# An output projection as two Strassen chunks in the feed-forward's order, its sums from DRAM

## The chip, the cores and the metric

The kernel runs on one NeuronCore of one Trainium2 chip. A NeuronCore has five engines that run side by side, each with its own queue of instructions in order: TensorE (PE, matrix products into PSUM; its weight loads are shown apart as PEld), VectorE (DVE), ScalarE (ACT), GpSimd (POOL) and SyncE (SP), which here only issues DMAs. They wait for each other by semaphores. The metric is the device time of one execution in microseconds (us), as a median of several runs.

## What is computed

A block of a recurrent network on x of 8 batches x 1024 tokens x 512 features, all in fp32:

```python
xn = _layernorm(x, axis=-1)
# attention part, for each batch, scale = 128 ** -0.5
local_out  = softmax(q k^T * scale) v                 # full attention, 128 features
sparse_out = the same, with only the 102 largest scores of a row kept
x_proj     = xn @ memory_proj_w
mem_out    = concat(x_proj, softmax(x_proj bank^T) bank) @ mem_out_w + mem_out_b
pred_out   = gelu((xn @ pred_in_w + pred_in_b) @ pred1_w + pred1_b) @ pred2_w + pred2_b
combined   = concat([local_out, sparse_out, mem_out, pred_out])   # 512 features
s = combined @ warboss_w + warboss_b                  # the output projection
# feed-forward part
g = silu(relu(xn @ w1 + b1) @ w2 + b2)                # 512 -> 2048 -> 512
out = x + s * g
```

The output projection is a product of (tokens x 512) with a weight of 512 x 512.

## The kernel before

**Units of work.** A tile i is 128 tokens, a pair p two tiles (256 tokens, `T`), a group g two pairs. There are 64 tiles, 32 pairs and 16 groups. Attention goes by tiles and pairs, the feed-forward by groups (w1) and pairs (w2).

**Strassen products.** The feed-forward's two products, the q and k projections and the projection `m` (the inputs of memory and prediction heads) are already computed by a Strassen scheme of the Winograd form: both operands are cut into 2 x 2 blocks, 4 sums of blocks are made on each side, 7 products of blocks take the place of 8, and additions put the results together. The sums of the weights are made once by `form_chunk` (L483), written to DRAM, and then read by `load_chunk` (L460) as a chunk of 7 blocks of 128 x 256 numbers (896 KB) into a ring `w` of four buffers. While the weights are raw, the fourth raw block lies in a separate tile, `raw_blocks` (L457). An "up" chunk (w1) is 14 matmuls of 256 columns, a "down" chunk (w2) 7. The left sums of the hidden values are made on POOL by `hidden_sums` (L597, tile hs), at most three chunks ahead; the additions after the products are `add_products` (L508): two of 128x512 and three of 128x256 elements. `use_units` (L548) calls it for the units (up, q, k, m) on POOL and then passes the result on through ACT. At most two units are open (tile u has two buffers). `make_gate` (L618) does it for a pair's w2 product (tile m), adds b2 and applies SiLU.

**The planner.** Which instruction comes when on each engine is laid down when the program is built. `run` (L132) keeps a clock for each engine in columns of TensorE. Attention and all follow-up work are generators ("chains") that yield the clock or the condition at which they go on. Where no chain is due, the next piece of the filler is issued: `feed_forward` (L634) goes through the chunks in the fixed order of `plan` (L400). A chunk that isn't ready holds the whole filler. Chains are sorted by rank: hidden sums -1, units 0, attention 1, the gate and the end of a pair 2. Chains for the n-th tile start at `begin + n * STEP` (L1024, L1034). The order is fixed on each engine, so on the chip an instruction can wait for one before it on its own engine.

**The order of a group.** For g: up g,0 to up g,7; among the first four the second half of the previous odd pair (down 2g-1,4 to 7), among the last four down 2g,0 to 3, and m after up g,2. Then down 2g,4 to 7 and down 2g+1,0 to 3, with the q (and k) chunk of the next group among them. The chunk `down n,7` waits until pair n-1 is "gated".

**The output projection before.** `finish_pair` (L923) takes a pair whose heads are done: LOCAL and SPARSE attention (`attend`, L753) and the memory and prediction heads (2 and 3, started by `two_heads`, L1047). It borrows two tiles of the pool `ws` (`borrow`, L207, 512 KB each), loads warboss_w into them and x into xr on SP's queue, waits for the last head, and runs for each of two token tiles four matmuls of 512 columns into po. ACT copies po to o, POOL adds the bias wb; later, when the gate is there, POOL multiplies, adds x and stores. `joined` is set after the products; the next pair's attention and small heads wait for it (`before_pair`, L766), because each head has one buffer. wk and wq of the start, and each batch's wv, are borrowed from `ws` as well.

Nearly all instructions are issued through one helper (L85), so the profile's rows are told apart by their tiles: f is the w2 product in PSUM, ph_up the w1 product, po the output projection, pa an attention's product with v, sc its scores, pp the prediction head, ptx and ptp transposes.

Of the kernel before, what the change touches and what calls it, by code (L numbers as in the profile page):

```python
# [20 lines left out]
def kernel(  # L21
# [182 lines left out]
    def can_borrow(n):  # L204
        return lambda: lent[0] + n <= 2

    def borrow(name, *parts):  # L207
        lent[0] += 1
        t = sb.tile([P, ND, 2 * HD], F32, tag="ws", name=name, bufs=2)
        at = 0  # L210
        for w in parts:
            v = w.rearrange("(c p) n -> p c n", p=P)
            if v.shape[1] == ND:
                sp.dma_start(out=t[:, :, at : at + v.shape[2]], in_=v)
                at += v.shape[2]
            else:
                t = t.rearrange("p c n -> p (c n)").rearrange("p (c n) -> p c n", n=v.shape[2])
                sp.dma_start(out=t, in_=v)
        return t

    def give_back(n=1):
        lent[0] -= n
# [4 lines left out]
    def borrow_qkv(name, which):  # L227
        return borrow(name, *[w[:, which * HD : (which + 1) * HD] for w in qkv])
# [3 lines left out]
    first_k = borrow_qkv("wk_0", 1)  # L232
# [91 lines left out]
    def ln_apply(b, j, t):  # L324

        mv, rs = stats[b]
        dve.tensor_scalar(t, t, mv[:, j, 0:1], rs[:, j : j + 1], ALU.subtract, ALU.mult)
        on("dve", 330)
        return after("dve")
# [70 lines left out]
    def plan():  # L400

        half = NWC // 2
        for g in range(GROUPS + 1):
            for k in range(NWC):
                if g < GROUPS:
                    yield "up", g, k
                if k >= half and g < GROUPS:  # L410
                    yield "down", 2 * g, k - half
                if k < half and g:
                    yield "down", 2 * g - 1, k + half
                if k == 2 and g < GROUPS:
                    yield "m", g, 0
                if g == 0 and k in (3, 5):
                    yield "form", "qk"[k // 4], 0
            if g < GROUPS:
                for n in range(2):
                    for k in range(half):  # L420
                        yield "down", 2 * g + n, k + half * (1 - n)
                        if g + 1 < GROUPS:
                            at = n * half + k
                            if (g + 1) % NG == 0:
                                if at == 2:
                                    yield "k", g + 2, 0
# [9 lines left out]
        for kind in ("up", "down", "q", "k", "m")  # L436
        for k in range(NWC if kind in ("up", "down") else 1)
# [3 lines left out]
    w2v = ffn_w2.rearrange("(h k p) n -> p h k n", h=2, p=P)  # L441

# [14 lines left out]
    raw_blocks = sb.tile([P, 7, H], F32, tag="m", name="raw_blocks")  # L457
    formed = set()

    def load_chunk(at):  # L460
        if at >= len(order_of_chunks):
            return
        kind, n, k = order_of_chunks[at]
        w = sb.tile([P, 7, H], F32, tag="w", name=f"w_{kind}_{n}_{k}", bufs=4)
        w_tiles[kind, n, k] = w
        what = n if kind == "form" else kind
        if (what, k) in formed:
            sp.dma_start(out=w, in_=w_dram[what, k])
            return
        formed.add((what, k))  # L470
        extra = raw_blocks[:, at % 7]
        raw[at] = what, extra
        if what == "down":
            for slot, h, d in ((0, 0, 0), (1, 1, 0), (6, 1, 1)):
                sp.dma_start(out=w[:, slot], in_=w2v[:, h, k, ts(d, H)])
            sp.dma_start(out=extra, in_=w2v[:, 0, k, H:])
        else:
            u1, u2 = blocks(what, k)
            for slot, v in ((0, u1[:, 0]), (1, u1[:, 1]), (4, u2[:, 1])):
                sp.dma_start(out=halves(w[:, slot]), in_=v)  # L480
            sp.dma_start(out=halves(extra), in_=u2[:, 0])

    def form_chunk(at):  # L483

        if at not in raw:
            return
        kind, n, k = order_of_chunks[at]
        what, extra = raw.pop(at)
        w = w_tiles[kind, n, k]
        if what == "down":  # L490
            on_pool("tensor_sub", w[:, 5], extra, w[:, 0])
            on_pool("tensor_sub", w[:, 2], w[:, 6], w[:, 5])
            on_pool("tensor_sub", w[:, 3], w[:, 6], extra)
            on_pool("tensor_sub", w[:, 4], w[:, 1], w[:, 2])
        else:
            on_dve("tensor_add", w[:, 5], extra, w[:, 4])
            on_dve("tensor_sub", w[:, 2], w[:, 5], w[:, 0])
            on_dve("tensor_sub", w[:, 3], w[:, 0], extra)
            on_dve("tensor_sub", w[:, 6], w[:, 1], w[:, 2])
        sp.dma_start(out=w_dram[what, k], in_=w)  # L500
# [91 lines left out]
    starts = {}  # L592
    units_begun = [0]
    sums_made = [0]
    downs_made = [0]

    def hidden_sums():  # L597

        for _, n, k in [c for c in order_of_chunks if c[0] == "down"]:
            yield lambda: (n, k) in hidden and sums_made[0] < downs_made[0] + 3  # L600
            yield after("act", 0)
            h = hidden.pop((n, k))
            a11, a21, a12, a22 = (h[:, u, ts(j, P)] for u in range(2) for j in range(2))
            s = sb.tile([P, 4, P], F32, tag="hs", name=f"hs_{n}_{k}", bufs=3)
            on_pool("tensor_add", s[:, 0], a21, a22)
            on_pool("tensor_sub", s[:, 1], s[:, 0], a11)
            on_pool("tensor_sub", s[:, 2], a11, a21)
            on_pool("tensor_sub", s[:, 3], a12, s[:, 1])
            operands[n, k] = (a11, a12, s[:, 1], s[:, 2], a22, s[:, 0], s[:, 3])
            sums_made[0] += 1  # L610
            due = after("pool")
            wanted_at[n, k] = due
# [4 lines left out]

    def make_gate(n, m):  # L618
        add, free = (on_dve, lambda: True) if n == LAST else (on_pool, pool_is_free)
# [14 lines left out]
    def feed_forward():  # L634

        sums = []
        for at, (kind, n, k) in enumerate(order_of_chunks):
            if kind == "form":
# [5 lines left out]
                continue  # L644
            if kind != "down":
# [4 lines left out]
                    and n in tokens  # L650
# [16 lines left out]
            for i in range(7):  # L667
                if kind != "down":
                    if i % 2 == 0:
                        ps = ring(f"ph_{kind}_{n}_{k}_{i}", (P, 2, T))  # L670
                    for c in range(2):
                        pe.matmul(
                            ps[:, i % 2], halves(w[:, i])[:, c], tokens[n][i][:, c],
                            start=c == 0, stop=c == 1,
                        )
# [247 lines left out]
    def finish_pair(b, p):  # L923
        yield needs(*[("head", b, p, h) for h in (LOCAL, 2, 3)])
        if (b, p) != (0, 0):
            yield needs(("out", *divmod(b * NP + p - 1, NP)))
        yield can_borrow(2)
        both = [borrow(f"wb_{b}_{p}_{k}", warboss_w[ts(k, T), :]) for k in range(2)]
        xs = [load_x("xr", b, 2 * p + j, "xr") for j in range(2)]
        yield clock["pe"] + AHEAD  # L930
        yield needs(("head", b, p, SPARSE))
        yield after("act")
        order = (LOCAL, 2, 3, SPARSE)
        os = []
        for j in range(2):
            ps = ring(f"po_{b}_{p}_{j}", (P, D))
            accumulate(
                ps,
                [heads[b, p, h][:, ts(j, P)] for h in order],
                [both[h // 2][:, h % 2, :] for h in order],  # L940
                D,
            )
# [7 lines left out]
        yield needs(("gate", b, p))  # L950
        yield after("act")
        late = b * NP + p == LAST
        op, free = (on_dve, lambda: True) if late else (on_pool, pool_is_free)
# [70 lines left out]
    STEP = int(0.995 * (12031 + NWC * (2 * 7 * T + 2 * 7 * H) // 4))  # L1024
# [5 lines left out]
    give_back()  # L1030
# [3 lines left out]
    for n in range(B * NT):  # L1034
# [57 lines left out]
```

## Time and profile before

| | |
|---|---|
| median of 3 runs | 2952.89 us (2951.46 to 2952.97) |
| the profiled execution | 2952.86 us, its span 2951.1 us |
| granted TensorE clock | 0.998 of full speed |
| VectorE: MAX8 and MATCH_REPLACE8 (sparse selection) | 943.1 + 850.5 us in the two largest rows |
| POOL: additions on u_up | 330.3 us (x256 of 128x512, 1290 ns) + 292.9 us (x384 of 128x256, 763 ns) |
| POOL: hs<-h of 128x128 | 245.2 us (x512, 479 ns) |
| TensorE: po<-wb,head of 128x512 | x512, 593 ns each by the page, 230.1 us busy |
| ACT: o<-po of 128x512 | x64, 585 ns |
| DMA | 512.60 MB, mean 174 GB/s; SP's queue 48.0% of the 16 engines |
| DMA wb (warboss_w) | x64, 512 KB, 6.4 us from issue to landing |
| DMA w_down | x248, 896 KB, 4.6 us from issue to landing |

How to read it: a row of the profile names an engine, an operation, output and input tiles, shapes, the number of instructions, busy time and the mean of one. Ends of matmuls are modelled and overlap the next one's start, so the mean duration (593 ns) isn't the spacing. A row of waits reads "engine tile <- the one that released it: total us, times, longest us". The page's slices cut the span into 40 equal parts and give the busy share of each in tenths.

### The profile page before, as it was taken

The page shows a single profiled execution, that of the slowest core. Times are in us where ns is not written, and L with a number is a line of the kernel's source. Part 1 is how long each engine was busy: PE and PEld are TensorE (multiplying, and loading weights), DVE is VectorE, ACT ScalarE, POOL GpSimd, SP SyncE. Part 2 cuts the span into 40 slices and gives each one's busy share as a digit, 9 for nine tenths or more (in the row PEclk, how much of TensorE's full clock was granted, in tenths as well). Part 3 has the DMA queues.
Part 4 walks back from the last instruction along what each step waited for, and adds up shares of the span by engine and source line. Part 5 has one row for each costly group of instructions (what it writes and reads, how often), then busy time and mean ns, then how long its engine had stood idle before and what let it go on. Part 6 is the DMA issues. An engine that isn't in the chain of part 4 may idle for free.

```text
span 2951.1 us, 37099 instructions
## 1 busy us (share of the span) xinstructions
PE 2881.2 (98%) x12912; PEld 2322.4 (79%) x12912; DVE 2369.6 (80%) x3181; ACT 1641.4 (56%) x3106; POOL 1937.4 (66%) x2499
## 2 busy tenths in 40 slices
PE   8999999999999999999999999999999999999998
PEld 5867878777887788778788778787888778777786
DVE  6999878887778787879869787788958979589595
ACT  3556555555565654556546565465654656446463
POOL 3775765767657676566857658576685766847665
PEclk9999999999999999999999999999999999999999
DMA  5764543645436455453554545455444554444544
GB/s 163 252 224 154 185 178 120 219 152 189 174 122 227 142 191 184 146 193 139 191 175 168 190 141 180 175 179 185 154 173 163 195 185 149 175 147 169 179 175 148
DMA packets 139035, 512.60 MB, mean 174 GB/s; under 512 B 13662, under 2 KB 39280, under 8 KB 138848
## 3 DMA queue, kind: packets, MB, share of 16 engines
q1 hardware_dynamic: 133392, 493.01, 48.0%
q0 software_dynamic: 5456, 17.22, 1.6%
q8 instruction: 102, 1.67, 0.2%
q14 instruction: 85, 0.70, 0.1%
HBM read 475.97 MB, written 34.21 MB: 173 GB/s over the span
## 4 chain that ended last, share of the span: by engine, by line
PE 81%; DVE 8%; ACT 5%; POOL 2%; DMA 1%; issue 1%; SPq 0%; POOLq 0%; DVEq 0%; ACTq 0%
PE ph_up L85 22%; PE f L85 21%; PE pa L85 7%; PE po L85 7%; PE sc L85 6%; PE pv L85 4%; PE ptp L85 3%; DVE top L85 3%; DVE left L85 3%; PE ph_m L85 3%; PE ph_k L85 2%; PE ph_q L85 2%; PE pp L85 1%; ACT L85 1%; ACT h L85 1%
## 5 line engine op out<-in xcount | busy, mean ns | idle before, releaser
L85 DVE MAX8 top<-left 128x8 f32<-128x1024 f32 x768 | 943.1, 1228 | 26.7
L85 DVE MATCH_REPLACE8 left<-top,left 128x1024 f32<-128x1024 f32 x704 | 850.5, 1208 | 0.0
L85 POOL TENSOR_TENSOR u_up<-u_up 128x256 f32<-128x256 f32 (+1 forms) x640 | 619.9, 974 | 329.9 <-ACT u_up L85 304.5
L85 PE MATMUL f<-w_down,hs 128*128 128x256 f32 x2048 | 540.8, 381 | 3.8 <-POOL w_down L85 3.1
L85 PE MATMUL ph_up<-t,w_up 128*128 128x256 f32 x2048 | 483.2, 380 | 0.0
L85 PEld LDWEIGHTS f<-w_down,hs 128*128 128x128 f32 x2048 | 383.9, 191 | 71.0 <-issue 18.8
L85 PEld LDWEIGHTS ph_up<-t,w_up 128*128 128x128 f32 x2048 | 385.1, 191 | 65.2 <-issue 17.9
L85 PE MATMUL f<-w_down,h 128*128 128x256 f32 x1536 | 423.9, 381 | 4.8 <-DMA w_down<-w_down_dram 2.3
L85 ACT COPY u_up<-ph_up 128x512 f32<-128x512 f32 (+1 forms) x512 | 264.1, 530 | 238.3 <-PE ph_up L85 237.4
L85 PE MATMUL ph_up<-xnT,w_up 128*128 128x256 f32 x1536 | 383.3, 380 | 1.1 <-ACT el L85 0.9
L85 POOL TENSOR_TENSOR hs<-h 128x128 f32<-128x128 f32 x512 | 245.2, 479 | 164.7 <-PE f L85 144.4
L85 PEld LDWEIGHTS f<-w_down,h 128*128 128x128 f32 x1536 | 287.6, 191 | 57.3 <-issue 15.7
L85 PEld LDWEIGHTS ph_up<-xnT,w_up 128*128 128x128 f32 x1536 | 288.3, 191 | 45.2 <-issue 8.1
L85 DVE MAX8 top<-s 128x8 f32<-128x1024 f32 x64 | 78.3, 1224 | 268.6 <-ACT s L85 268.6
L85 PE MATMUL sc<-kT,qT 128*128 128x512 f32 x512 | 241.6, 595 | 4.1 <-ACT u_up L85 1.9
L85 PE MATMUL pa<-pT,v 128*128 128x256 f32 x1024 | 231.9, 380 | 0.6 <-ACT pT L85 0.6
L85 PE MATMUL po<-wb,head 128*128 128x512 f32 x512 | 230.1, 593 | 0.0
L85 ACT ACTIVATE h<-u_up,biasT 128x256 f32<-128x256 f32 x512 | 219.7, 501 | 8.4 <-POOL u_up L85 8.4
L85 POOL TENSOR_TENSOR o<-o,wb 128x512 f32<-128x512 f32 x64 | 81.5, 1273 | 217.4 <-ACT o L85 217.1
L85 PEld LDWEIGHTS pa<-pT,v 128*128 128x128 f32 x1024 | 194.8, 190 | 27.1 <-ACT pT L85 1.2
L85 ACT COPY pT<-ptp 128x512 f32<-128x512 f32 x256 | 148.5, 586 | 116.1 <-PE ptp L85 115.3
L85 POOL TENSOR_TENSOR m<-m 128x256 f32<-128x256 f32 (+1 forms) x155 | 152.1, 989 | 64.0 <-ACT m L85 59.6
(151 smaller groups left out, 4150.3 us busy)
## 6 DMA issues: line engine op xcount, KB each, us to landing
w_down<-w_down_dram SPq DMA_DIRECT2D x248, 896.0 KB, 4.6
w_up<-w_up_dram SPq DMA_DIRECT2D x120, 896.0 KB, 4.6
wb<-in_L_attn_warboss_w_dram SPq DMA_DIRECT2D x64, 512.0 KB, 6.4
xl<-in_L_attn_x_dram SPq DMA_DIRECT2D x64, 256.0 KB, 4.6
xr<-in_L_attn_x_dram SPq DMA_DIRECT2D x64, 256.0 KB, 2.9
out_dram<-xr POOLq DMA_DIRECT2D x62, 256.0 KB, 2.8
xs<-in_L_attn_x_dram SPq DMA_DIRECT2D x56, 256.0 KB, 4.8
w_q<-w_q_dram SPq DMA_DIRECT2D x15, 896.0 KB, 4.6
```

The lines of the kernel that those rows point to most:

```text
L85: r = made(*args, **kwargs)
```

## The change

The output projection becomes two chunks of kind "po" in the filler's order, each 7 products of 128x128 by 128x256 numbers (e = 0 for the heads 0 and 2, e = 1 for the heads 1 and 3), both summed in PSUM. A pair's po stands after `down n,5` for an even pair (after `down 1,1` for the first) and after `down n,7` for an odd one. The weight's sums come from DRAM like those of the other weights; they are made once, on DVE. `finish_pair` makes the left sums of the heads on POOL and waits for the results; `use_units` does the additions and adds the bias, on POOL, for the last pair on DVE.

Besides: the raw blocks of all weights are loaded into their own chunk and one is overwritten in place (`raw_blocks` is gone); `ws` has one buffer, and wk of the start lies in the memory of el; the q and k weights' sums are formed at other places; `two_heads` waits for ACT before its first matmul; the statistics of the second batch start a step later; the planner allows 500 columns where it allowed 330 for the normalization of a tile; STEP is shorter by 0.995 x 256 columns.

```diff
     def can_borrow(n):
-        return lambda: lent[0] + n <= 2
+        return lambda: lent[0] + n <= 1
...
-        t = sb.tile([P, ND, 2 * HD], F32, tag="ws", name=name, bufs=2)
+        t = sb.tile([P, ND, 2 * HD], F32, tag=tag, name=name)
...
-    first_k = borrow_qkv("wk_0", 1)
+    first_k = borrow_qkv("wk_0", 1, "el")
...
         dve.tensor_scalar(t, t, mv[:, j, 0:1], rs[:, j : j + 1], ALU.subtract, ALU.mult)
-        on("dve", 330)
+        on("dve", 500)
...
-                if g == 0 and k in (3, 5):
-                    yield "form", "qk"[k // 4], 0
+                if k == half - 1 and g:
+                    for e in range(2):
+                        yield "po", 2 * g - 1, e
+                if (g, k) in ((0, 5), (1, 4)):
+                    yield "form", "qk"[g], 0
             if g < GROUPS:
                 for n in range(2):
                     for k in range(half):
                         yield "down", 2 * g + n, k + half * (1 - n)
+                        if (n, k) == (int(g == 0), 1):
+                            for e in range(2):
+                                yield "po", 2 * g, e
...
+    wbv = warboss_w.rearrange("(h k p) n -> p h k n", h=2, p=P)
...
-    raw_blocks = sb.tile([P, 7, H], F32, tag="m", name="raw_blocks")
...
-        if what == "down":
-            for slot, h, d in ((0, 0, 0), (1, 1, 0), (6, 1, 1)):
-                sp.dma_start(out=w[:, slot], in_=w2v[:, h, k, ts(d, H)])
-            sp.dma_start(out=extra, in_=w2v[:, 0, k, H:])
+        if what in ("down", "po"):
+            v = w2v if what == "down" else wbv
+            for slot, h, d in ((0, 0, 0), (1, 1, 0), (3, 0, 1), (6, 1, 1)):
+                sp.dma_start(out=w[:, slot], in_=v[:, h, k, ts(d, H)])
...
+        if what in ("down", "po"):
+            on = on_pool if what == "down" else on_dve
+            on("tensor_sub", w[:, 5], w[:, 3], w[:, 0])
+            on("tensor_sub", w[:, 2], w[:, 6], w[:, 5])
+            on("tensor_sub", w[:, 3], w[:, 6], w[:, 3])
+            on("tensor_sub", w[:, 4], w[:, 1], w[:, 2])
...
     def use_units(kind, g, k, m, nth):
-        for _ in add_products(m, on_pool):
-            yield pool_is_free
+        add, free = engine_for(g if kind == "po" else 0)
+        for _ in add_products(m, add):
+            yield free
+        if kind == "po":
+            n = g
+            if n:
+                yield needs(("out", *divmod(n - 1, NP)))
+            os = outs[n] = []
+            for j, blocks in enumerate((m[:, 1:7:5], m[:, 4:6])):
+                o = sb.tile([P, D], F32, tag="o", name=f"o_{n}_{j}", bufs=2)
+                add("tensor_add", halves(o), blocks, halves(wb))
+                os.append(o)
+                yield free
+            done.add(("units", nth))
+            return
...
+    def left_sums(h1, h2, s):
+
+
+        a11, a21, a12, a22 = (h[:, ts(j, P)] for h in (h1, h2) for j in range(2))
+        on_pool("tensor_add", s[:, 0], a21, a22)
+        on_pool("tensor_sub", s[:, 1], s[:, 0], a11)
+        on_pool("tensor_sub", s[:, 2], a11, a21)
+        on_pool("tensor_sub", s[:, 3], a12, s[:, 1])
+        return (a11, a12, s[:, 1], s[:, 2], a22, s[:, 0], s[:, 3])
...
+    def engine_for(n):
+        return (on_dve, lambda: True) if n == LAST else (on_pool, pool_is_free)
...
+            if kind == "po" and k == 0:
+                wants[0] = lambda: True
+                yield 0
+                load_chunk(at + 3)
+                form_chunk(at + 1)
+                continue
...
                     "constants" in done
-                    and n in tokens
+                    and (
+                        ("po", n) in operands and wanted_at["po", n] <= clock["pe"]
+                        if kind == "po"
+                        else n in tokens
+                    )
                     and (nth < 2 or ("units", nth - 2) in done)
...
-            load_chunk(at + 3)
+            if kind != "po":
+                load_chunk(at + 3)
             form_chunk(at + 1)
             w = w_tiles.pop((kind, n, k))
+            if kind == "po":
+                both = [(w_tiles.pop((kind, n, 0)), w)]
+                both = [(x[:, i], y[:, i]) for x, y in both for i in range(7)]
...
+                        if kind == "po":
+                            lhsT, rhs = operands[kind, n][c][i], both[i][c]
+                        else:
+                            lhsT, rhs = halves(w[:, i])[:, c], tokens[n][i][:, c]
+                        pe.matmul(ps[:, i % 2], lhsT, rhs, start=c == 0, stop=c == 1)
                         yield T
...
                 start(use_units(kind, n, k, m, nth), rank=0)
+                if kind == "po":
+                    load_chunk(at + 3)
+                    operands.pop((kind, n))
+                    done.add(("joined", *divmod(n, NP)))
...
     def finish_pair(b, p):
-        yield needs(*[("head", b, p, h) for h in (LOCAL, 2, 3)])
-        if (b, p) != (0, 0):
-            yield needs(("out", *divmod(b * NP + p - 1, NP)))
-        yield can_borrow(2)
-        both = [borrow(f"wb_{b}_{p}_{k}", warboss_w[ts(k, T), :]) for k in range(2)]
+        n = b * NP + p
+        yield needs(*[("head", b, p, h) for h in range(4)], *before_pair(b, p))
+        yield after("act", 0)
+        sums = sb.tile([P, 2, 4, P], F32, tag="ho", name=f"ho_{n}")
+        operands["po", n] = []
+        for e in range(2):
+            operands["po", n].append(
+                left_sums(heads.pop((b, p, e)), heads.pop((b, p, e + 2)), sums[:, e])
+            )
+            wanted_at["po", n] = after("pool", 100000 * (1 - e))
+            yield after("pool", 0)
+        wanted_at["po", n] = after("pool")
+        if n:
+            yield needs(("out", *divmod(n - 1, NP)))
         xs = [load_x("xr", b, 2 * p + j, "xr") for j in range(2)]
-        yield clock["pe"] + AHEAD
-        yield needs(("head", b, p, SPARSE))
+        yield lambda: ("gate", b, p) in done and len(outs.get(n, ())) == 2
         yield after("act")
-        order = (LOCAL, 2, 3, SPARSE)
-        os = []
-        for j in range(2):
-            ps = ring(f"po_{b}_{p}_{j}", (P, D))
-            accumulate(
-                ps,
-                [heads[b, p, h][:, ts(j, P)] for h in order],
-                [both[h // 2][:, h % 2, :] for h in order],
-                D,
-            )
-            o = sb.tile([P, D], F32, tag="o", name=f"o_{b}_{p}_{j}", bufs=2)
-            copy(o, ps, 360)
-            on_pool("tensor_add", o, o, wb)
-            os.append(o)
-            yield pool_is_free
-        give_back(2)
-        done.add(("joined", b, p))
...
-    STEP = int(0.995 * (12031 + NWC * (2 * 7 * T + 2 * 7 * H) // 4))
+    STEP = int(0.995 * (11775 + NWC * (2 * 7 * T + 2 * 7 * H) // 4))
...
-                start(prepare_stats(b + 1), now + 2000)
+                start(prepare_stats(b + 1), now + (2000 if b else STEP))
...
                 yield needs(("m", b, p), *before_pair(b, p))
+                yield after("act")
```

More of the change, by code (lines that the diff above doesn't have):

```diff
@@ L204, in can_borrow, with borrow @@
     def can_borrow(n):
-        return lambda: lent[0] + n <= 2
-    def borrow(name, *parts):
-        lent[0] += 1
-        t = sb.tile([P, ND, 2 * HD], F32, tag="ws", name=name, bufs=2)
+        return lambda: lent[0] + n <= 1
+    def borrow(name, *parts, tag="ws"):
+        lent[0] += tag == "ws"
+        t = sb.tile([P, ND, 2 * HD], F32, tag=tag, name=name)
         at = 0
@@ L212, in borrow, with give_back, borrow_qkv @@
             v = w.rearrange("(c p) n -> p c n", p=P)
[L213 to L218, printed above, removed]
-        return t
-    def give_back(n=1):
-        lent[0] -= n
+            sp.dma_start(out=t[:, :, at : at + v.shape[2]], in_=v)
+            at += v.shape[2]
+        return t
+    def give_back():
+        lent[0] -= 1
     qkv = (local_qkv_w, sparse_qkv_w)
     AHEAD = 8000
-    def borrow_qkv(name, which):
-        return borrow(name, *[w[:, which * HD : (which + 1) * HD] for w in qkv])
+    def borrow_qkv(name, which, tag="ws"):
+        return borrow(name, *[w[:, which * HD : (which + 1) * HD] for w in qkv], tag=tag)
     first_x = [load_x("xl", 0, j, ("o", "xr")[j // 2]) for j in range(4)]
-    first_k = borrow_qkv("wk_0", 1)
+    first_k = borrow_qkv("wk_0", 1, "el")
     for h in range(2):
@@ L435 @@
         (kind, k): dram.tile([P, 7, H], F32, tag=f"{kind}_{k}", name=f"w_{kind}_{k}_dram")
-        for kind in ("up", "down", "q", "k", "m")
-        for k in range(NWC if kind in ("up", "down") else 1)
+        for kind, ks in (("up", NWC), ("down", NWC), ("po", 2), ("q", 1), ("k", 1), ("m", 1))
+        for k in range(ks)
     }
@@ L470, in load_chunk @@
         formed.add((what, k))
-        extra = raw_blocks[:, at % 7]
-        raw[at] = what, extra
-        if what == "down":
-            for slot, h, d in ((0, 0, 0), (1, 1, 0), (6, 1, 1)):
-                sp.dma_start(out=w[:, slot], in_=w2v[:, h, k, ts(d, H)])
-            sp.dma_start(out=extra, in_=w2v[:, 0, k, H:])
+        raw[at] = what
+        if what in ("down", "po"):
+            v = w2v if what == "down" else wbv
+            for slot, h, d in ((0, 0, 0), (1, 1, 0), (3, 0, 1), (6, 1, 1)):
+                sp.dma_start(out=w[:, slot], in_=v[:, h, k, ts(d, H)])
         else:
             u1, u2 = blocks(what, k)
-            for slot, v in ((0, u1[:, 0]), (1, u1[:, 1]), (4, u2[:, 1])):
+            for slot, v in ((0, u1[:, 0]), (1, u1[:, 1]), (3, u2[:, 0]), (4, u2[:, 1])):
                 sp.dma_start(out=halves(w[:, slot]), in_=v)
-            sp.dma_start(out=halves(extra), in_=u2[:, 0])
     def form_chunk(at):
@@ L487, in form_chunk @@
         kind, n, k = order_of_chunks[at]
-        what, extra = raw.pop(at)
+        what = raw.pop(at)
         w = w_tiles[kind, n, k]
[L490 to L494, printed above, removed]
+        if what in ("down", "po"):
[4 more added lines that the diff above has]
+            on("tensor_sub", w[:, 4], w[:, 1], w[:, 2])
         else:
-            on_dve("tensor_add", w[:, 5], extra, w[:, 4])
+            on_dve("tensor_add", w[:, 5], w[:, 3], w[:, 4])
             on_dve("tensor_sub", w[:, 2], w[:, 5], w[:, 0])
-            on_dve("tensor_sub", w[:, 3], w[:, 0], extra)
+            on_dve("tensor_sub", w[:, 3], w[:, 0], w[:, 3])
             on_dve("tensor_sub", w[:, 6], w[:, 1], w[:, 2])
@@ L592 @@
     starts = {}
+    outs = {}
     units_begun = [0]
@@ L602, in hidden_sums @@
             h = hidden.pop((n, k))
-            a11, a21, a12, a22 = (h[:, u, ts(j, P)] for u in range(2) for j in range(2))
             s = sb.tile([P, 4, P], F32, tag="hs", name=f"hs_{n}_{k}", bufs=3)
[L605 to L609, printed above, removed]
+            operands[n, k] = left_sums(h[:, 0], h[:, 1], s)
             sums_made[0] += 1
@@ L616 @@
     LAST = B * NP - 1
+    def engine_for(n):
+        return (on_dve, lambda: True) if n == LAST else (on_pool, pool_is_free)
     def make_gate(n, m):
-        add, free = (on_dve, lambda: True) if n == LAST else (on_pool, pool_is_free)
+        add, free = engine_for(n)
         for _ in add_products(m, add):
@@ L671, in feed_forward @@
                     for c in range(2):
-                        pe.matmul(
-                            ps[:, i % 2], halves(w[:, i])[:, c], tokens[n][i][:, c],
-                            start=c == 0, stop=c == 1,
-                        )
+                        if kind == "po":
[3 more added lines that the diff above has]
+                        pe.matmul(ps[:, i % 2], lhsT, rhs, start=c == 0, stop=c == 1)
                         yield T
@@ L923, in finish_pair @@
     def finish_pair(b, p):
-        yield needs(*[("head", b, p, h) for h in (LOCAL, 2, 3)])
-        if (b, p) != (0, 0):
-            yield needs(("out", *divmod(b * NP + p - 1, NP)))
-        yield can_borrow(2)
-        both = [borrow(f"wb_{b}_{p}_{k}", warboss_w[ts(k, T), :]) for k in range(2)]
+        n = b * NP + p
[12 more added lines that the diff above has]
+            yield needs(("out", *divmod(n - 1, NP)))
         xs = [load_x("xr", b, 2 * p + j, "xr") for j in range(2)]
-        yield clock["pe"] + AHEAD
-        yield needs(("head", b, p, SPARSE))
+        yield lambda: ("gate", b, p) in done and len(outs.get(n, ())) == 2
         yield after("act")
-        order = (LOCAL, 2, 3, SPARSE)
-        os = []
-        for j in range(2):
-            ps = ring(f"po_{b}_{p}_{j}", (P, D))
-            accumulate(
-                ps,
-                [heads[b, p, h][:, ts(j, P)] for h in order],
-                [both[h // 2][:, h % 2, :] for h in order],
-                D,
-            )
-            o = sb.tile([P, D], F32, tag="o", name=f"o_{b}_{p}_{j}", bufs=2)
-            copy(o, ps, 360)
-            on_pool("tensor_add", o, o, wb)
-            os.append(o)
-            yield pool_is_free
-        give_back(2)
-        done.add(("joined", b, p))
[L950 to L953, printed above, removed]
+        late = n == LAST
+        op, free = engine_for(n)
+        os = outs.pop(n)
         for j, o in enumerate(os):
@@ L1029 @@
         project_k(0, g, LOCAL, first_k)
-    give_back()
     begin = clock["pe"] + 2000
```

## Prediction

> **What bounds the kernel now.** I read the page's busy shares first, then the row of slices, the chain that ended last, and the timeline of TensorE. The busy shares and the slices:
>
> ```profile
> PE 2881.2 (98%) x12912; PEld 2322.4 (79%) x12912; DVE 2369.6 (80%) x3181; ACT 1641.4 (56%) x3106; POOL 1937.4 (66%) x2499
> ...
> PE   8999999999999999999999999999999999999998
> ...
> PE 81%; DVE 8%; ACT 5%; POOL 2%; DMA 1%; issue 1%; SPq 0%; POOLq 0%; DVEq 0%; ACTq 0%
> ```
>
> TensorE is busy in every slice and carries 81% of the chain (third line). The Trainium skill warns against taking that at its word: "Perfetto Trace Analysis", section "Identifying the Most-Contended Engine", calls matmul busy time a bad measure and would judge by weight loads. Those are 79%, beside VectorE's 80% (first line). By that rule TensorE has a fifth in hand and fewer columns might buy nothing. So I look at starts instead of ends, in the timeline of TensorE (start, duration, instruction, count):
>
> ```profile
> 164.58 3.60 PE L85 MATMUL po<-wb,head 128*128 128x512 f32 x8
> ...
> 168.01 0.59 PE L85 MATMUL f<-w_down,hs 128*128 128x256 f32 x2
> ...
> 1469.93 3.62 PE L85 MATMUL pa<-pT,v 128*128 128x256 f32 x16
> 1473.38 2.75 PE L85 MATMUL ph_k<-t,w_k 128*128 128x256 f32 x12
> ```
>
> From the first po to the next f, 3.43 us for 8 instructions: 0.429 us per 512 columns. From pa to ph_k, 3.45 us for 16: 0.216 us per 256 columns. An fp32 matmul is two such instructions (po has 512 = 32 pairs x 8 matmuls x 2). Taking 0.429, 0.216, 0.109 and 0.06 us for the instructions of 512, 256, 128 and 64 columns, the trace's TensorE work sums to 2848 us; the starts exceed it by 83 us in all; 9.7 us lie before the first and 9.6 after the last. **The columns bound it**: the trace decides against the rule. A column removed is worth 0.84 ns per instruction as long as the rest keeps pace.
>
> **The output projection on TensorE.** Removed per pair: 2 x 4 matmuls of 512 columns, 16 instructions x 0.429 = 6.87 us. Added: 7 products x 2 chunks of 256 columns, 28 x 0.216 = 6.05 us. Saved 0.82 us a pair, **26.3 us** over 32. Weight loads rise from 16 to 28 a pair; one lasts 191 ns (the po and pa rows), so it fits under 216 ns, with 25 ns to spare where it had 238. The pa and f rows already run at that spacing, so I charge nothing. If that cover were gone, 12 loads x 0.19 us would be 2.3 us a pair and the gain would turn.
>
> **The same product on the other engines.** Per pair POOL gains 8 left sums of 128x128 (479 ns in the hs row: 3.83 us), 2 adds of 128x512 (1.29 us) and 3 of 128x256 (0.76 us): 4.87 us. The two bias adds (1.27 us) stay. 8.7 us x 32 = 278 us, so POOL goes from 1937 to some 2215 us, 66% to 76%. ACT copies four products' tiles (3 x 0.58 + 0.38) where it copied two (2 x 0.585): +0.95 us a pair, 56% to 58%. Here a rule speaks against the change: "GPSIMD Engine Reference", section "Engine selection", puts elementwise work on VectorE, GpSimd being about 2x slower with two inputs. The trace agrees: 128x512 m<-m takes 1278 ns on POOL and 691 on DVE. By the rule the additions belong on VectorE, where 8.7 us would be about 4.6; but VectorE would then stand at 80% + 5%, in front of the selection rounds, and the price on POOL counts only where TensorE waits for POOL. TensorE's waits show how little that is now:
>
> ```profile
> PE ptx L85 <- DVE xl L85: 19.0, 14, 9.7
> PE pp L85 <- ACT xh L85: 11.1, 12, 1.4
> ...
> PE f L85 <- POOL w_down L85: 3.1, 1, 3.1
> ...
> PE f L85 <- DMA w_down<-w_down_dram: 2.3, 1, 2.3
> ...
> PE f L85 <- POOL hs L85: 0.8, 1, 0.8
> ```
>
> (Columns: total us, times, longest.) POOL's own order also loses a blockage, since the bias add no longer stands at its head waiting for a product just issued:
>
> ```profile
> POOL u_up L85 <- ACT u_up L85: 304.5, 101, 30.6
> ...
> POOL o L85 <- ACT o L85: 217.1, 53, 12.8
> ```
>
> Where can POOL be late? Counting 28 instructions to an up chunk and 14 to a down chunk, I find each chunk's start. Hidden sums end some 10 to 60 us before their chunk, but twice in a group only 1 to 6 us. A chunk's additions and ReLUs end 10 to 16 us after its matmuls, and in the second half of the up loop only 2 to 5 us before the unit after next, because at most two unit tiles are open. po is one more unit, with 7.5 us on POOL against an up chunk's 4.9 us. So the late stretch is after an odd pair's po: up 4 and up 5 have one down chunk less (3.0 us) ahead of them. The nearest row is the memory chunk m, which stands between up chunks in just this way: ph_up's starts exceed their spacing by only 2.7 us in the whole run. Bounds: below, minus 2 us (the blockage gone reaches a few chunks); above, 7.5 - 4.9 = 2.6 us a pair, 84 us. I take the value near the row, 0.25 us a pair: **+8 us**.
>
> **Order and waits.** po stands at a fixed place of the filler. I compared that place with the copies of both attention heads (head<-pa): the chunk before it ends 30 to 98 us after the second head, except for the last pair (6 us). The left sums (3.8 us) fit, so po does not stall the filler. po now comes 12 to 64 us later than before, and `joined` with it. Behind `joined` wait the next pair's two small heads and its attentions. For even pairs these slip 10 to 20 us (pair 16's small heads began at 1563.0, its predecessor's po would end near 1583), yet their own po is 30 us or more off, and the filler runs meanwhile: nothing lost. On ACT the head copies move with them. The gate's wait (`gated` before the next down 7) had some 40 us in hand; about 10 of them go.
>
> The small heads also wait for ACT now, and for `joined`, which for even pairs comes after their input. The wait of pp for xh (11.1 us above) was paid once a group, on the spot; I expect it gone, **-11 us** (ends 0 and -15.8, all excess before pp). What is late next there is the Gelu, 0.5 us in all. The longer allowance for a normalized tile moves a transpose 170 columns (0.28 us) later; 13 of its 14 waits (9.3 us; the one of 9.7 lies at the start) shrink by at most 3.7: **-3 us**.
>
> **DMA and SP.** wb's 64 loads of 512 KB become 64 of 896 KB: +25 MB on 513, 48% to about 50% of the queues' time. SP's issues keep their number. But po takes two ring tiles, and the load three chunks on is issued only when its matmuls end, so two chunks lie ready instead of three. After an even pair's po these are two downs, 6.05 us of TensorE; w_down lands in 4.6 us. It fits unless SP stands at an xr load: SP waited 246.4 us in 54 times for out_dram, 4.6 us each. Ends: 0, and (4.6 + 4.6 - 6.05) x 16 = 50 us; I take 0, as xr's loads come after `out`, tens of us off, and charge it to a rival.
>
> **One answer together.** Weights' sums in place, k and q formed at other places, wk in el's memory, one ws buffer, statistics a step later: once each, on engines that wait anyway; between -3 us (the 3.1 us wait for w_down near 150 us) and +3 us (8 sums for po on DVE, 0.8 us each, in a queue of 2.4 us rounds). I take 0. STEP shrinks by 255 columns, which follows the work and isn't a second gain. The tail: from the last head (2929.0 us) it was 6 us of f, 6.9 of po, then copy, bias, product, sum and the store. After: sums under the same f, 6.05 of po, a copy of 256 columns and DVE adds of 0.4 to 0.7 us. Equal within 1 us.
>
> **The sum.** -26.3 - 11 - 3 + 8 = -32.3. The profiled execution took 2952.86 us (span 2951.1 and 1.8 around it), like the median, 2952.89. So **2921 us**; with the ends of the unknowns near their rows, 2906 to 2934.
>
> **Rivals.**
> - Only the columns count (chance 0.18): the slipped attentions bunch, and new waits eat what pp and ptx give. For it: `joined` falls up to 24 us after the time at which the LOCAL attention now runs (pair 24). Against it: the filler covers. 2952.9 - 26.3 + 8 = 2935; up to 2946 with another 11.
> - POOL becomes late (0.05), after each po. For it: 20 us windows of POOL in the trace reach 98%. Against: its average stays near 76%, and m's row. 2921 - 8 + 84 = 2997. It ends on the other side from 1.3 us lost a pair (40/32).
> - The ring runs dry after even pairs' po (0.04): 2921 + 50 = 2971, from 2.0 us a time.
> - The change removes no time because weight loads set the pace at 256 columns (0.03): against it stand the pa and f rows. About 2950.
>
> My own case has 0.70. Below 0.2% (5.9 us) a measurement of this kernel can't be told from no change. Faster (under 2947): 0.86, my case and 0.16 of the first rival; within: 0.05, its rest and the last; slower: 0.09, the two between. The range goes from 2904 (all of pp's 15.8 us, no new wait) to 2945.
>
> **What would show it.** po as 896 products' instructions at 0.216 us and 6.05 us a pair; pp's wait for xh gone from TensorE's list; POOL near 2215 us and still few waits of PE for POOL hs; `POOL o <- ACT o` gone; f's waits for w_down's DMA still a few us. I am wrong if f or ph_up wait tens of us for POOL or DMA, if weight loads exceed 191 ns, or if TensorE's excess of starts grows past 83 us.

## The result, and the profile after

The changed kernel takes 2927.41 us (median of 4 runs, 2925.8 to 2928.97) beside 2952.93 us of the kernel before (4 runs): a ratio of 0.9915, 95% interval 0.9897 to 0.9932, or 25.5 us less. Forecast were 32 us less, with a range of 2904 to 2945 us. The profiled execution took 2925.8 us, its span 2923.7.

From the page of the changed kernel: the busy shares, a group of POOL's additions, and the row of the w_po loads (number of loads, KB each, median us from issue to landing):

```profile
PE 2856.1 (98%) x13296; PEld 2395.7 (82%) x13296; DVE 2379.2 (81%) x3196; ACT 1668.8 (57%) x3169; POOL 2184.0 (75%) x2908
...
L85 POOL TENSOR_TENSOR u_po<-u_po 128x256 f32<-128x256 f32 (+1 forms) x155 | 148.2, 963 | 18.5 <-ACT u_po L85 12.1
...
w_po<-w_po_dram SPq DMA_DIRECT2D x62, 896.0 KB, 4.7
```

POOL grew by 247 us, weight loads to 82%, and TensorE is as full as it was. What it waits for has changed. Its waits in the changed kernel, first five and the row of pp (total us, times, longest us):

```profile
PE ph_po L85 <- DMA w_po<-w_po_dram: 15.0, 11, 2.1
PE ptx L85 <- DVE xl L85: 11.9, 4, 10.0
PE ptp L85 <- ACT es L85: 7.3, 3, 5.3
PE f L85 <- ACT h L85: 5.8, 2, 4.7
PE pa L85 <- ACT pT L85: 4.4, 4, 1.3
...
PE pp L85 <- ACT pT L85: 0.8, 1, 0.8
```

The wait of pp for xh (11.1 us before) is gone, and ptx waits 4 times instead of 14. At the head stands a new one: the output projection waits for its own weights.

A second view adds up. I take each TensorE instruction's distance to the next one's start, subtract the spacing of its shape (0.429, 0.216, 0.108, 0.06 us for 512, 256, 128, 64 columns) and sum what exceeds it by more than 40 ns, by the instruction that came late:

| us | before | changed kernel |
|---|---|---|
| columns at their spacing | 2847.8 | 2821.9 |
| excess, all | 82.7 | 82.0 |
| of it ahead of pp | 15.8 | 1.1 |
| ahead of ptx | 13.9 | 5.8 |
| ahead of ph_po (po before) | 0.1 | 22.7 |

The time went down by about the columns (25.5 us by the medians, 25.9 us of columns). The two small gains came, 22.9 us together, and the new excess at ph_po took 22.7 us. So the changed kernel gained what the columns alone give, as in the first rival ("only the columns count"), but for another cause and without that rival's 8 us for POOL: it had 2935 us.

**Where ph_po waits.** Counting 28 instructions to a pair, all of the excess lies at even pairs, and but for 0.1 us in 7 of the 16 (4, 8, 10, 12, 16, 22, 26). 16.8 us of it stand ahead of the first matmul of each of the two chunks. One of the seven, pair 8, in the timelines of SP's queue and of TensorE, and in SP's waits between 868 and 895 us:

```profile
877.52 4.15 SPq L85 DMA_DIRECT2D xr<-in_L_attn_x_dram  x2
881.76 0.38 SPq L85 DMA_DIRECT2D xs<-in_L_attn_x_dram  x1
882.24 0.86 SPq L85 DMA_DIRECT2D w_po<-w_po_dram  x2
```

```profile
885.51 1.03 PE L85 MATMUL f<-w_down,hs 128*128 128x256 f32 x4
888.61 0.67 PE L85 MATMUL ph_po<-w_po,head 128*128 128x256 f32 x2 [2.07 <-DMA w_po<-w_po_dram]
890.69 2.93 PE L85 MATMUL ph_po<-w_po,head 128*128 128x256 f32 x6 [1.42 <-DMA w_po<-w_po_dram]
```

```profile
SPq L85 <- DMA out_dram<-xr: 10.8, 2, 7.4
```

SP stands at the two xr loads, whose buffers the stores of the pair before still read: 7.4 us ahead of the first, which leaves at 877.52, and 3.4 ahead of the second, 10.8 us in all. (The 4.15 us of the row run from the first one's start to the second one's end.) Behind them both w_po loads are ready to go and leave one right after the other, at 882.24 and 882.72. One matmul (two instructions) after the first chunk, the second is needed as well. Six of the seven cases show the same rows, SP at xr and then both w_po loads at once; SP's stand at a pair's xr loads was 8.9 to 13.0 us in the seven. In pair 10 two w_down loads leave at once behind xr, and w_po after them.

**A part of it is the clock.** Two stretches of pair 8 (start and end, length, busy us of PE, PEld, DVE, ACT and POOL with their instructions, then granted TensorE clock, DMA share, GB/s):

```profile
877.00:894.00 17.00, 13.52 (x54) 10.84 (x53) 10.36 (x15) 2.81 (x6) 12.75 (x15) 0.90 0.80 291
892.00:894.00 2.00, 2.00 (x6) 1.55 (x6) 0.00 (x0) 0.29 (x1) 0.00 (x0) 0.50 0.93 370
```

Behind the wait the granted clock was 0.50 for 3.4 us, and the matmuls started every 0.427 us instead of 0.216. The same happened in pairs 12 and 22, and in none of the other four. These three pairs had waited longest, 2.8 to 3.8 us within one po, the others up to 2.3 us. The slow matmuls are some 5 of ph_po's 22.7 us.

### The profile page after: what moved, and what is told of

It reads as the page before. It is cut to its first block, busy times and chain, and to the rows that moved or that the text cites. A ratio compares the mean times of both kernels' runs of the same rounds, so it can differ in the third digit from the quotient of the medians.

```text
span 2923.7 us, 38478 instructions
## 1 busy us (share of the span) xinstructions
PE 2856.1 (98%) x13296; PEld 2395.7 (82%) x13296; DVE 2379.2 (81%) x3196; ACT 1668.8 (57%) x3169; POOL 2184.0 (75%) x2908
## 5 line engine op out<-in xcount | busy, mean ns | idle before, releaser
L85 POOL TENSOR_TENSOR u_up<-u_up 128x256 f32<-128x256 f32 (+1 forms) x640 | 618.1, 972 | 247.8 <-ACT u_up L85 223.1
L85 DVE TENSOR_REDUCE nml<-el 128x1 f32<-128x1024 f32 x64 | 77.4, 1209 | 231.3 <-ACT el L85 231.0
L85 ACT ACTIVATE h<-u_up,biasT 128x256 f32<-128x256 f32 x512 | 219.6, 501 | 11.2 <-POOL u_up L85 11.1
L85 POOL TENSOR_TENSOR u_po<-u_po 128x256 f32<-128x256 f32 (+1 forms) x155 | 148.2, 963 | 18.5 <-ACT u_po L85 12.1
```

Of the source, the lines that this page charges most:

```text
L85: r = made(*args, **kwargs)
```

## The experiments

The kernel before was run again beside each group of experiments, with medians between 2951.5 and 2954.3 us, and ratios are against these runs. "Excess" is the sum of the table above.

### xr's loads moved away

```diff
             yield needs(("out", *divmod(n - 1, NP)))
+            yield clock["pe"] + 6000
         xs = [load_x("xr", b, 2 * p + j, "xr") for j in range(2)]
```

> The changed kernel with one line more: finish_pair waits 6000 columns (10 us) after the previous pair's `out` before it puts its xr loads on SP's queue. Theory (SP stands at xr until out_dram has landed, and the w_po loads queue behind it): SP's wait for DMA out_dram falls from 247.8 us to under 60, PE's excess of starts before ph_po falls from 22.7 us to under 8, and the time falls by 12 to 18 us, to about 2911. Rival (two po chunks at once are simply more than a ring with two chunks of lead can bring, whatever SP does): SP's wait for out_dram falls, but ph_po's excess stays at 15 to 23 us and the time within 4 us of 2927.

Measured: 2905.28 us, ratio 0.984 (0.9825 to 0.9854), 22 us less than the changed kernel. SP's wait for out_dram fell from 247.8 us to 32.0, and ph_po vanished from TensorE's waits, whose head now reads:

```profile
PE ptx L85 <- DVE xl L85: 11.8, 4, 9.9
PE ptp L85 <- ACT es L85: 7.0, 3, 5.1
PE f L85 <- ACT h L85: 5.8, 2, 4.7
```

The order of TensorE's 13,296 instructions is the same as in the changed kernel, instruction by instruction, and so is that of DVE, ACT and POOL. The excess is 61.0 us in all: ph_po's is gone, the other rows together stand at 61.0 where they had 59.3. The three stretches at half the clock are gone with it. SP's queue around pair 8, with the same columns as above:

```profile
874.79 5.06 SPq L85 DMA_DIRECT2D w_po<-w_po_dram  x2
882.55 0.32 SPq L85 DMA_DIRECT2D w_down<-w_down_dram  x1
882.97 0.86 SPq L85 DMA_DIRECT2D xr<-in_L_attn_x_dram  x2
```

The w_po loads leave first and one after the other, as their buffers come free; the two xr loads take 0.86 us of SP instead of 4.15. The ring with its two chunks of lead is enough when nothing stands in the queue; what made it late was the queue. The gain went 4 us past the top of what was expected, because all 22.7 us of excess went, the slow matmuls with the waits, and not two thirds of it.

### The same move in the kernel before

```diff
-        xs = [load_x("xr", b, 2 * p + j, "xr") for j in range(2)]
         yield clock["pe"] + AHEAD
+        xs = [load_x("xr", b, 2 * p + j, "xr") for j in range(2)]
```

> The kernel before with its xr loads issued 8000 columns (13 us) later, behind the wait that stands there anyway. Theory (SP's stand was harmless while each chunk was used one at a time with three chunks of lead; it costs only since po takes two at once): SP's wait for out_dram falls from 246.4 us to under 80, and the time stays within 4 us of 2951. Rival (SP's stand cost before as well): 5 to 20 us faster.

Measured: 2949.8 us beside 2954.29, ratio 0.9985 (0.9978 to 0.9991): 4.5 us less, with SP's wait for out_dram down to 9.5 us. The excess fell from 82.7 to 78.9 us: f's 2.3 us for w_down and little else. The order of every engine but SP is unchanged here too. A small part of the rival holds: SP's stand cost some 4 us before too. In the new order it costs 22 us. That the two chunks taken at once make this difference is the likely reason, but no run changes that alone.

### An even pair's po behind a unit

The rows of `plan` that yield an even pair's po move behind the q chunk (even groups) or the k chunk (odd groups):

```diff
-                        if (n, k) == (int(g == 0), 1):
...
+                        if n * half + k == (5 if g == 0 else 2 if g % 2 else 3):
+                            for e in range(2):
+                                yield "po", 2 * g, e
```

> The changed kernel with an even pair's po one place later, right behind the q chunk (even groups) or the k chunk (odd groups), so that 9.1 us of TensorE's work instead of 6.05 lie between the issue of po's second load and its use; xr's loads stay. Ring theory (lead is what lacks): ph_po's excess falls from 22.7 us to under 6, time 2908 to 2914. SP theory (an xr load of 4 us in front of them is what makes them late): about 3 us more of lead cover most of each wait of 1.6 to 2.3 us if SP still stands there; excess under 10 us, time 2912 to 2920. Neither: 2927.

Measured: 2938.26 us, ratio 0.995 (0.9934 to 0.9967): slower than the changed kernel by 11 us and outside all three expectations. The wait itself went, 0.07 us of excess is left at ph_po, although SP still waited 200.4 us for out_dram. So more lead removes it too, and this run doesn't tell the two theories apart. But the whole order was laid anew, and the excess rose to 93.4 us elsewhere: f from 11.8 to 26.3, ptp from 14.5 to 28.3, sc from 3.7 to 8.2. Of these the profile names only parts (ptp for ACT es 12.2 us, f for ACT m 5.3, f for w_down's DMA 2.6). It isn't the clock, whose mean is 0.995 where the changed kernel had 0.994. Why this order waits so much more stays open. It shows that a place in the filler can't be judged by the wait that it removes.

### The small edits alone, in the kernel before

```diff
-        on("dve", 330)
+        on("dve", 500)
...
                 yield needs(("m", b, p), *before_pair(b, p))
+                yield after("act")
```

> The kernel before with only two of the change's small edits: `yield after("act")` in two_heads and 500 columns instead of 330 for a tile's normalization. Theory (these two terms are real and independent of po): pp's excess falls from 15.8 us to under 3 and ptx's waits of PE for DVE from 19.0 us to about 12 to 15, and the time falls by 11 to 16 us, to 2937 to 2942. Rival (waits removed in one place come back in another, since the order of all engines is laid anew): the total excess of PE's starts over their spacing stays near 83 us and the time within 5 us of 2953.

Measured: 2935.76 us beside 2951.5, ratio 0.9943 (0.9928 to 0.9957): 15.7 us less. The excess before pp fell from 15.8 to 2.7 us, before ptx from 13.9 to 7.1, in all from 82.7 to 65.8, although ptp rose from 8.8 to 20.4. The two edits together are worth this without po; the run doesn't part them, and the time fell 1 us below the expected 2937 to 2942.

### Without the wait for ACT in the small heads

```diff
                 yield needs(("m", b, p), *before_pair(b, p))
-                yield after("act")
```

> The changed kernel without `yield after("act")` in two_heads. Theory: the wait of pp for xh went because `joined` now comes after the input of the even pairs' small heads, so it stays away without that line: under 3 us before pp, time within 4 us of 2927. Rival: the line itself removed it, and 10 to 15 us before pp come back: 2937 to 2942.

> The kernel with the later xr loads and without `yield after("act")` in two_heads. Theory (the 7 us that this line's removal gained came from fewer waits of ph_po for its weights, 15.0 us of excess where there were 22.7): with the xr loads away nothing is left of that, 2901 to 2908. Rival (the line costs by itself, in the order it lays): another 5 to 8 us go, to about 2898.

Measured in the changed kernel: 2920.21 us (ratio 0.989, 0.9876 to 0.9905), 7 us faster than with the line, where one theory had 2927 and the other 2937 to 2942. The excess before pp is 3.4 us: most of the wait stays away without the line. The traces show why: in the kernel before, pp's first matmul started 0.1 us after xh in 14 of the 16 even pairs; here it starts 0.2 us after the start of the previous pair's last po instruction in 14 of them, and 8.6 to 11.2 us after xh. So `joined` is what it waits for now. Either reason can remove most of the 11 us: the line did in the kernel before (with the longer allowance beside it), `joined` does here. Of the time, ph_po's excess gave most: it is 15.0 us here and 22.7 with the line, while other rows rose by some 3 us. With xr's loads away, the line's removal gives nothing (2907.83 us, ratio 0.9841, 0.9827 to 0.9856, where the kernel with the line has 0.984): that is inside the 2901 to 2908 us of the theory, and the rival (2898) falls.

### The longer allowance undone

With the later xr loads, 330 columns again:

> The kernel with the later xr loads and 330 columns again for a tile's normalization. Theory (the 170 columns took 3 us from ptx's waits): excess before ptx rises from 5.8 us to 9 to 14 and the time by 2 to 6 us, to about 2909. Rival (in the new order nothing depends on it): within 2 us of 2905.

Measured: 2903.23 us, ratio 0.9836 (0.9819 to 0.9852): not told apart from 0.984, and the excess before ptx is 5.7 us, as with 500 columns. So in the new order ptx's waits didn't go by the allowance; what is left is the order itself, which no run isolates.

### More work on POOL

With the later xr loads, POOL makes the left sums and bias adds twice; the planner isn't told, so all orders but POOL's stay:

```diff
         on_pool("tensor_sub", s[:, 3], a12, s[:, 1])
+        if again:
+            pool.tensor_add(s[:, 0], a21, a22)
...
                 add("tensor_add", halves(o), blocks, halves(wb))
+                if n != LAST:
+                    pool.tensor_add(halves(o), blocks, halves(wb))
```

> The kernel with the later xr loads, in which POOL makes a pair's left sums and the two bias adds twice, into the same tiles and without a word to the planner, so that only POOL's work grows: 8 x 0.46 + 2 x 1.28 = 6.2 us a pair, 197 us in all, from 75% to 82% of the span. Theory (TensorE doesn't wait for POOL): the time stays within 10 us of 2905 and PE's waits for POOL below 5 us. Rival (POOL stands close to the path after po, so what the change adds there already costs): at least a fifth of the added work shows, 40 us or more, and waits of PE for POOL hs or for ACT h behind POOL appear.

Measured: 2911.34 us, ratio 0.9855 (0.984 to 0.987); the interval overlaps that of the kernel without the extra work, and the time is within the 10 us expected. Its page and TensorE's two first waits:

```profile
PE 2852.0 (98%) x13296; PEld 2392.1 (82%) x13296; DVE 2387.3 (82%) x3196; ACT 1671.5 (57%) x3169; POOL 2375.2 (82%) x3226
...
PE ptx L85 <- DVE xl L85: 11.3, 4, 9.4
PE f L85 <- ACT h L85: 9.3, 2, 8.3
```

193 us more on POOL raise the excess by 7.6 us, from 61.0 to 68.6, of which 3.5 us are one wait of f for h at the start (9.3 where it was 5.8). TensorE's order is the same in both. So about one part in 25 of POOL's added work reaches TensorE.

### po's additions on DVE

```diff
-        add, free = engine_for(g if kind == "po" else 0)
+        add, free = engine_for(LAST if kind == "po" else 0)
```

> The kernel with the later xr loads, with po's additions and bias on DVE for all pairs instead of for the last one: POOL loses 7.5 us a pair (232 us, to some 67%), DVE gains 4.1 us a pair (126 us, to some 86%). Theory (neither is on the path): 2900 to 2912. The rule that elementwise work belongs on VectorE would make it faster by 5 us or more; the rival that DVE's selection rounds are nearer to the path makes it slower by 5 us or more, with longer waits of PE behind DVE (ptp for ACT es, ptx for DVE xl).

Measured: 2913.39 us, ratio 0.9861 (0.9846 to 0.9876), with POOL at 1989.2 us (68%) and DVE at 2530.6 us (87%). Not faster, and 1 us above the range of the theory: by the ratios it is 6 us slower, with intervals that overlap by a sliver. The excess is 68.7 us instead of 61.0, with ptp's wait for ACT es at 10.9 us where it was 7.0, as the rival about the selection rounds expects. But some 5 of these 7.7 us are matmuls at half the granted clock (its mean is 0.994 here, 0.997 without this edit), so what the move itself costs stays open. DVE's gain by addition was smaller than 0.69 us against 1.28 promised: the 128x512 additions on u_po took 692 ns in the median but 903 in the mean. The 29 that ran beside POOL's additions for more than half of their time took 1.16 us, the 33 beside none 0.69. POOL lost 193 us, DVE gained 155.

### Left sums only when POOL is free

With the later xr loads:

```diff
         for e in range(2):
+            yield pool_is_free
             operands["po", n].append(
```

> The kernel with the later xr loads, in which finish_pair waits until POOL's clock is free before each half of a pair's left sums. Theory (the longest wait left, 4.7 us of f for ACT h near 162 us, comes from the first pair's left sums, which stand on POOL ahead of an up chunk's last addition while the down weights are formed): this wait goes, and the time falls by 3 to 6 us, to about 2901. Rival (POOL is full there anyway): the wait stays within 1 us and the time within 3 us of 2905; a late order of left sums elsewhere could cost as much.

Measured: 2915.65 us, ratio 0.9876 (0.9861 to 0.989), slower by 10 us, where the theory had 2901 and the rival 2905. f's wait for h fell from 5.8 to 2.3 us as expected, and f waits 3.9 us for POOL hs instead; but the order is a new one from there on, and the excess ahead of ptp alone grew from 14.1 to 23.5 us.

## Why the prediction was right, and where it was not

- **What bounds the kernel**: right. The columns fell by 25.9 us (forecast 26.3), the time by 25.5, and the excess stayed (82.0 us, 82.7 before). In all twelve profiles the excess is only 59 to 93 us of the span, beside some 20 us before the first and after the last instruction; the rest is columns at their spacing.
- **Columns against weight loads**: right. ph_po starts every 0.216 us (median of 895), loads last 190 ns. The trace, not the share of weight loads, told what a column is worth. (The Trainium skill, "Perfetto Trace Analysis", section "Identifying the Most-Contended Engine", names MFU, the matmul work done as a share of the peak, beside that share; the prediction used the share alone.)
- **POOL**: busy 2184 us for a forecast 2215. I took +8 us. The rows that I had in mind show nothing of it: f and ph_up together have 14.0 us of excess where they had 16.3. But the run with more work on POOL lost 7.6 us of excess for 193 us of work; at that rate, an estimate, the change's 247 us would be some 10, near my price. The price is small; between these it stays open. The engine-selection rule that the prediction cites brought no gain in the run on DVE.
- **pp**: forecast -11, measured -14.8 us of excess ahead of it. Either of the two reasons given (the line and `joined`) removes most of it.
- **ptx**: forecast -3, measured -8.1 us; but the mechanism I gave, 170 columns of allowance, does nothing in the new order (5.7 us without it, 5.8 with it).
- **DMA and SP: the step that failed.** I wrote "It fits unless SP stands at an xr load" and then "I take 0, as xr's loads come after `out`, tens of us off". It measured +22.7 us, inside the ends of 0 and 50 that I had set. Some 17 us of it are waits for w_po, some 5 the half clock behind them, for which I had no term. Two things were wrong in the step. The xr loads are not tens of us off: for an even pair, `out` of the pair before comes just ahead of its po (in pair 8 the first xr load left 9 us before po was due, and SP had stood at it since 870). And I looked for the late chunk behind po, at the load that is issued when po ends; late were po's own two loads, needed one matmul apart after a lead of two down chunks.
- **The place of po, the tail, the heads**: right; no wait of ph_po for heads or left sums on the list, and the time from TensorE's last start to the end is 8.9 us where it was 9.7.

That the forecast of 2921 is only 6 us off is partly luck. Set against the rows, pp gave 3.8 us more than forecast and ptx 5.1, and POOL's 8 don't show: 16.9 together. The fourth term, put at nothing, cost 22.7. Rows that the forecast has no term for moved as well and nearly cancelled: ptp and pa rose by 10.1 us, sc, pms, ptm and pk fell by 9.0.

The kernel with the later xr loads, 2905.28 us, is faster than both (1.6% under the kernel before); the one that also takes back the allowance is the same within its interval.

## What to carry to other kernels

When a step takes two buffers of a prefetch ring at once, write down for each of the two loads when it can leave and when it is used, and list every other instruction of the issuing queue that stands ahead of them: here one load that waited for a store held all that were behind it. A change of order moves small waits everywhere: here such sums lay between 59 and 93 us for the same work, so one removed wait is proven only by a run that keeps the order. And here an engine at 75% of its time, off the path, was worth no effort: 193 us more on it cost some 7 us, 193 us less gained nothing.

## What was not expected of the hardware

When both w_po loads of pair 8 left together, the first landed 6.2 us after its issue (at 888.47 us) and the second 7.9 us after its own (at 890.65), where the median w_po load lands after 4.7 us. With the xr loads moved away, pair 8's two landed after 4.9 and 4.4 us. In all eight pairs whose two loads left within half a microsecond, the first took 4.7 to 6.3 us and the second 6.4 to 8.3. The 17 us around this wait moved 291 GB/s, at 0.80 of the DMA engines' time (the row above), against a mean of 184 GB/s over the span. So the pause at xr was paid three times in pair 8: as a late start, as a crowd, and as 3.4 us of matmuls at half the granted clock. What sets the clock back wasn't tested; the stretches at half clock inside po came only behind its longest waits, and went with them.
